# A gather-and-matmul residual kernel: the scheduler's semaphores replaced by one section with semaphores written by hand, two for each of 23 slots

## The chip, the cores and the metric

The kernel runs on one core of a Trainium2 chip. The metric is device time in microseconds, the median of several runs. The engines named below are TensorE (PE, matmuls; PEld is its weight load), VectorE (DVE), ScalarE (ACT), GpSimd (POOL) and SyncE (SP). ACT and SP do no arithmetic here: they only issue DMA transfers, each into a queue of its own, and both queues are served by the same 16 DMA engines.

## The reference

```python
def reference(x, itok_B_0_7, L0_cond_weights):
    # x: (128, 128, 1024), itok: (128,), weights: (8, 128, 128)
    w = weights[subjects]                       # (128, 128, 128), one matrix per batch entry
    out = jnp.einsum('bct,bcd->bdt', x, w)
    return x + out
```

For each of the 128 batch entries one of eight 128 x 128 matrices is chosen by an index, the entry's 128 x 1024 block is multiplied by it, and the block itself is added. x is 64 MiB, and so is the output; the weights are 512 KB. Each byte of x is read once and each byte of the output written once.

## The kernel before

The kernel takes two batch entries at a time (G = 2). A tile `xt` of 128 partitions x 2 x 1024 float32 is 1 MiB; 64 such tiles go through the kernel. The pool `xpool` has 23 buffers (BUFS, line 26), which the text calls slots: tile i lies in slot i mod 23.

At the start ACT issues two transfers: the 128 indices into `given` (line 48) and all eight weight matrices into `w_all` (line 50). DVE turns the indices into `index` (lines 54 to 59). After that the loop of line 61 does, for each tile:

- SP issues the load of the tile (line 63).
- For each of the two entries, POOL reads the index into a register and copies the chosen matrix from `w_all` to a small tile `w` (line 74; eight buffers).
- PE multiplies in two halves of 512 columns into `ps` (line 77; 4 buffers[...]).
- DVE adds the product to the tile in place (line 84).
- ACT issues the store of the tile (line 85).

The loop is a Python loop, so the program is straight code. No wait is written in the source: the framework's scheduler (Tile) orders the instructions and puts in every semaphore. For the completion of transfers issued by SP and ACT it has eight counters. It hands them out in rotation to loads and stores alike, in the order that it has planned, and a transfer is not issued until the transfer before it on the same counter has landed. In the built program loads 0 to 4 wait for nothing; load 5 waits for load 0; load 6 waits for `w_all`; load 7 for load 2; load 8 for store 0, and so on: of the 64 loads all but the first five wait for a counter that some other transfer used. From load 23 on a load also waits for the DVE's work on the tile that was in its slot. A store waits for the two additions of its tile and for its own counter. As a sequencer works in order, a waiting load holds up all later loads behind it on SP, and a waiting store all later stores on ACT. At the end SP waits for all counters, and then all engines meet in a barrier.

Of the kernel before, what the change touches and what calls it, by code (L numbers as in the profile page):

```python
# [1 line left out]

# [4 lines left out]

F32 = mybir.dt.float32
ALU = mybir.AluOpType


G = 2

N = 512

BUFS = 23


@with_exitstack
def kernel(  # L30
    ctx: ExitStack,
    tc: tile.TileContext,
    x: bass.AP,
    subjects: bass.AP,
    weights: bass.AP,
    out: bass.AP,
):
    nc = tc.nc
    B, C, T = x.shape
    S, _, D = weights.shape  # L40

    const = ctx.enter_context(tc.tile_pool(name="const", bufs=1))
    xpool = ctx.enter_context(tc.tile_pool(name="xpool", bufs=BUFS))
    wpool = ctx.enter_context(tc.tile_pool(name="wpool", bufs=8))
    psum = ctx.enter_context(tc.tile_pool(name="psum", bufs=4, space=bass.MemoryType.PSUM))

    given = const.tile([1, B], mybir.dt.int32, name="given")
    nc.scalar.dma_start(given, subjects.rearrange("(o b) -> o b", o=1))
    w_all = const.tile([C, S, D], F32, name="w_all")
    nc.scalar.dma_start(w_all, weights.rearrange("s c d -> c s d"))  # L50

    near = const.tile([1, B], mybir.dt.int32, name="near")
    nc.vector.tensor_scalar(near, given, -S, S - 1, ALU.max, ALU.min)  # L55
    wrap = const.tile([1, B], mybir.dt.int32, name="wrap")
    nc.vector.tensor_scalar(wrap, near, 0, S, ALU.is_lt, ALU.mult)  # L57
    index = const.tile([1, B], mybir.dt.int32, name="index")
    nc.vector.tensor_tensor(index, near, wrap, ALU.add)  # L59

    for b0 in range(0, B, G):
        xt = xpool.tile([C, G, T], F32, name="xt")
        nc.sync.dma_start(xt, x[b0 : b0 + G].rearrange("g c t -> c g t"))  # L63
        for g in range(G):
            b = b0 + g
            s = nc.values_load(  # L66
                index[0:1, b : b + 1],
                engines=[mybir.EngineType.Pool],
                min_val=0,
                max_val=S - 1,  # L70
                skip_runtime_bounds_check_because="the index is clamped on the chip above",
            )
            w = wpool.tile([C, 1, D], F32, name="w")
            nc.gpsimd.tensor_copy(w, w_all[:, bass.ds(s, 1), :])  # L74
            ps = psum.tile([D, T], F32, name="ps")
            for t in range(0, T, N):
                nc.tensor.matmul(  # L77
                    ps[:, t : t + N],
                    w[:, 0, :],
                    xt[:, g, t : t + N],  # L80
                    start=True,
                    stop=True,
                )
            nc.vector.tensor_tensor(xt[:, g, :], ps, xt[:, g, :], ALU.add)  # L84
        nc.scalar.dma_start(out[b0 : b0 + G].rearrange("g d t -> d g t"), xt)


# [1 line left out]
_INS = ["x", "itok_B_0_7", "L0_cond_weights"]  # L89
_OUTS = [((128, 128, 1024), "float32")]  # L90


# [20 lines left out]
```

## Time and profile before

| | |
|---|---|
| median of 3 runs | 333.06 us (332.92 to 333.22) |
| the profiled execution | 333.28 us, of which the profile's span is 331.5 us |
| bytes moved by DMA | 134.88 MB, mean 407 GB/s |
| load of one tile, SP's issue to landing (line 63) | 4.9 / 19.9 / 27.8 us (least, median, most) |
| store of one tile, ACT's issue to landing (line 85) | 4.0 / 19.8 / 27.1 us |
| weights, issue to landing (line 50) | 16.3 us |
| one addition on DVE (line 84) | 1225 ns |
| one copy of a matrix on POOL (line 74) | 294 ns |
| first load issued, first store issued, last store issued | 0.74, 25.06, 317.9 us |

The page divides the span into 40 equal slices of 8.29 us. Per slice it gives a digit of busy tenths for each engine and the rate of all DMA in GB/s. A table by stretches gives the same for any stretch of time, with the time each engine was busy in it. A table of waits says for whom an engine, or an issuing sequencer (SPq, ACTq), waited, how long in total, how many times and at most. The chain of waits follows what ended last back to what released it. A wait for several semaphores is put down to the one that came last.

### The profile page before, as it was taken

The numbers are of one execution on the slowest core, as the hardware profiler recorded it, in microseconds if no ns is written. First come the engines' busy times: TensorE is split into PE (matmuls) and PEld (weight loads), VectorE is DVE, ScalarE is ACT, GpSimd is POOL, SyncE is SP. The second block draws the span as 40 slices with busy tenths as digits, with TensorE's granted clock in tenths as the row PEclk, the third lists the DMA queues.
The fourth block names the chain that finished last, engine by engine and source line by source line (L and its number), as shares of the span: only waits on it lengthen the run. The fifth ranks groups of instructions, "written<-read, shape, count | busy, mean of one in ns | idle before, by whom it ended". The sixth has DMA issues, their size and how long they took to land.

```text
span 331.5 us, 2130 instructions
## 1 busy us (share of the span) xinstructions
PE 235.4 (71%) x512; PEld 94.5 (29%) x512; DVE 157.5 (48%) x131; POOL 37.8 (11%) x132
## 2 busy tenths in 40 slices
PE   0089999978668668668668668667877687688620
PEld 0034444423223223223223223223323233233200
DVE  0027777754454454454454454453544544545420
POOL 0031111111111111111111111110111111110000
PEclk9999999999999999999999999998899999999975
DMA  7997999999999999999999999999999999999996
GB/s 283 392 401 270 376 421 421 422 418 421 421 419 421 422 420 420 420 421 420 420 422 421 420 421 421 419 422 418 422 421 422 420 421 419 421 420 421 420 421 261
DMA packets 35870, 134.88 MB, mean 407 GB/s; under 512 B 2065, under 2 KB 3090, under 8 KB 35858
## 3 DMA queue, kind: packets, MB, share of 16 engines
q10 hardware_dynamic: 18450, 67.64, 50.2%
q1 hardware_dynamic: 17408, 67.11, 49.8%
q8 instruction: 4, 0.07, 0.1%
q14 instruction: 8, 0.07, 0.0%
HBM read 67.63 MB, written 67.11 MB: 406 GB/s over the span
## 4 chain that ended last, share of the span: by engine, by line
PE 44%; DMA 32%; DVE 14%; issue 5%; SPq 0%; POOLq 0%; POOL 0%
PE ps L77 44%; DMA xt<-in_x_dram 30%; DVE xt L84 14%; DMA out_dram<-xt 2%; DMA given<-in_itok_B_dram 0%; SPq L63 0%; POOLq L66 0%; DVE index L59 0%; DVE wrap L57 0%; DVE near L55 0%; POOLq L74 0%; POOL w L74 0%
## 5 line engine op out<-in xcount | busy, mean ns | idle before, releaser
L77 PE MATMUL ps<-xt,w 128*128 128x512 f32 x512 | 235.4, 607 | 81.2 <-DVE xt L84 55.1
L84 DVE TENSOR_TENSOR xt<-ps,xt 128x1024 f32<-128x1024 f32 x128 | 156.7, 1225 | 158.3 <-PE ps L77 158.3
L77 PEld LDWEIGHTS ps<-xt,w 128*128 128x128 f32 x512 | 94.5, 192 | 221.3 <-issue 116.2
L74 POOL COPY w<-w_all 128x128 f32 x128 | 37.6, 294 | 260.7 <-PE ps L77 242.2
L55 DVE TENSOR_SCALAR near<-given 1x128 int32<-1x128 int32 x1 | 0.2, 215 | 2.0 <-DMA given<-in_itok_B_dram 2.0
L59 DVE CUSTOM_DVE_ANT_0 index<-near,wrap 1x256 uint16<-1x256 uint16 x1 | 0.3, 280 | 0.0
L57 DVE TENSOR_SCALAR wrap<-near 1x128 int32<-1x128 int32 x1 | 0.2, 216 | 0.0
L100 POOL MEMSET const-float32-0.0<- 128x1 f32 x1 | 0.1, 98 | 0.2 <-issue 0.2
L100 POOL MEMSET const-bfloat16-1.0<- 128x1 bf16 x1 | 0.1, 101 | 0.0
L100 POOL MEMSET const-uint8-127<- 128x1 uint8 x1 | 0.1, 101 | 0.0
L100 POOL MEMSET const-float32-1.0<- 128x1 f32 x1 | 0.1, 98 | 0.0
## 6 DMA issues: line engine op xcount, KB each, us to landing
xt<-in_x_dram SPq DMA_DIRECT2D x64, 1024.0 KB, 19.9
out_dram<-xt ACTq DMA_DIRECT2D x64, 1024.0 KB, 19.8
w_all<-in_L_cond_weights_dram ACTq DMA_DIRECT2D x1, 512.0 KB, 16.3
given<-in_itok_B_dram ACTq DMA_DIRECT2D x1, 0.5 KB
```

The costliest lines, as they stand in the source:

```text
L55: nc.vector.tensor_scalar(near, given, -S, S - 1, ALU.max, ALU.min)
L57: nc.vector.tensor_scalar(wrap, near, 0, S, ALU.is_lt, ALU.mult)
L59: nc.vector.tensor_tensor(index, near, wrap, ALU.add)
L74: nc.gpsimd.tensor_copy(w, w_all[:, bass.ds(s, 1), :])
L77: nc.tensor.matmul(ps[:, t : t + N], w[:, 0, :], xt[:, g, t : t + N], start=True, stop=True,)
L84: nc.vector.tensor_tensor(xt[:, g, :], ps, xt[:, g, :], ALU.add)
L100: nc = _bacc.Bacc("TRN2", target_bir_lowering=False, num_devices=1)
```

## The change

The whole of the work goes into one critical section: a block that the scheduler leaves as it is and in which all waits are written out. All tiles are allocated once, by name: 23 x tiles, 4 tiles for the chosen matrix (there were 8 buffers), 4 in PSUM. There are 52 semaphores: for each slot one for loads and one for stores, and six for the rest of the work.

- A load of slot k waits only for the store of the tile that was in that slot before (nothing, for the first 23). All 64 loads are issued on SP, as before.
- A store waits only until the two additions of its tile are done. All stores are issued on ACT, as before.
- PE waits for the load of its slot, for the copied matrix, and for the addition four entries ago. POOL waits for the product four entries ago. DVE waits for the product.
- At the end SP waits for the last store of each slot.
- The framework adds borders to the section: at its start all engines wait for an instruction of SP, at its end for another one, before the barrier that ends the kernel.

What is computed, the order of instructions on PE, DVE, POOL, SP and ACT, and the size of every transfer stay as they were.

```diff
-BUFS = 23
+SLOTS = 23
+W_SLOTS = 4
+P_SLOTS = 4
+DMA = 16
...
-    xpool = ctx.enter_context(tc.tile_pool(name="xpool", bufs=BUFS))
-    wpool = ctx.enter_context(tc.tile_pool(name="wpool", bufs=8))
-    psum = ctx.enter_context(tc.tile_pool(name="psum", bufs=4, space=bass.MemoryType.PSUM))
+    ws = [pool.tile([C, 1, D], F32, name=f"w{i}") for i in range(W_SLOTS)]
+    xs = [pool.tile([C, G, T], F32, name=f"x{i}") for i in range(SLOTS)]
+    ps = [psum.tile([D, T], F32, name=f"ps{i}") for i in range(P_SLOTS)]
...
+    s_load = [tc.alloc_semaphore(f"s_load{i}") for i in range(SLOTS)]
+    s_store = [tc.alloc_semaphore(f"s_store{i}") for i in range(SLOTS)]
+
+    with tc.tile_critical():
...
-    for b0 in range(0, B, G):
-        xt = xpool.tile([C, G, T], F32, name="xt")
-        nc.sync.dma_start(xt, x[b0 : b0 + G].rearrange("g c t -> c g t"))
+        for i in range(NT):
+            k, turn = i % SLOTS, i // SLOTS
+            if turn:
+                nc.sync.wait_ge(s_store[k], DMA * turn)
+            nc.sync.dma_start(
+                xs[k], x[i * G : (i + 1) * G].rearrange("g c t -> c g t")
+            ).then_inc(s_load[k], DMA)
+
+        nc.gpsimd.wait_ge(s_wall, DMA)
+        for i in range(NT):
+            k, turn = i % SLOTS, i // SLOTS
+            nc.tensor.wait_ge(s_load[k], DMA * (turn + 1))
+            for g in range(G):
...
+                if b >= W_SLOTS:
+                    nc.gpsimd.wait_ge(s_product, b - W_SLOTS + 1)
+                nc.gpsimd.tensor_copy(w, w_all[:, bass.ds(s, 1), :]).then_inc(s_copied, 1)
+
+                nc.tensor.wait_ge(s_copied, b + 1)
+                if b >= P_SLOTS:
+                    nc.tensor.wait_ge(s_added, b - P_SLOTS + 1)
...
+                nc.vector.wait_ge(s_product, b + 1)
...
-        nc.scalar.dma_start(out[b0 : b0 + G].rearrange("g d t -> d g t"), xt)
+            nc.scalar.wait_ge(s_added, (i + 1) * G)
+            nc.scalar.dma_start(
+                out[i * G : (i + 1) * G].rearrange("g d t -> d g t"), xs[k]
+            ).then_inc(s_store[k], DMA)
+
+        for i in range(NT - SLOTS, NT):
+            nc.sync.wait_ge(s_store[i % SLOTS], DMA * (i // SLOTS + 1))
```

More of the change, by code (lines that the diff above doesn't have):

```diff
@@ L18 @@
 F32 = mybir.dt.float32
+I32 = mybir.dt.int32
 ALU = mybir.AluOpType
@@ L40 @@
     S, _, D = weights.shape
-    const = ctx.enter_context(tc.tile_pool(name="const", bufs=1))
-    xpool = ctx.enter_context(tc.tile_pool(name="xpool", bufs=BUFS))
-    wpool = ctx.enter_context(tc.tile_pool(name="wpool", bufs=8))
-    psum = ctx.enter_context(tc.tile_pool(name="psum", bufs=4, space=bass.MemoryType.PSUM))
-    given = const.tile([1, B], mybir.dt.int32, name="given")
-    nc.scalar.dma_start(given, subjects.rearrange("(o b) -> o b", o=1))
-    w_all = const.tile([C, S, D], F32, name="w_all")
@@ L50 @@
[L50 to L59, printed above, removed]
-    for b0 in range(0, B, G):
-        xt = xpool.tile([C, G, T], F32, name="xt")
[L63 to L82, printed above, removed]
-                )
-            nc.vector.tensor_tensor(xt[:, g, :], ps, xt[:, g, :], ALU.add)
-        nc.scalar.dma_start(out[b0 : b0 + G].rearrange("g d t -> d g t"), xt)
@@ new lines @@
+    NT = B // G
+    pool = ctx.enter_context(tc.tile_pool(name="pool", bufs=1))
+    psum = ctx.enter_context(tc.tile_pool(name="psum", bufs=1, space=bass.MemoryType.PSUM))
+    given = pool.tile([1, B], I32, name="given")
+    near = pool.tile([1, B], I32, name="near")
+    wrap = pool.tile([1, B], I32, name="wrap")
+    index = pool.tile([1, B], I32, name="index")
+    w_all = pool.tile([C, S, D], F32, name="w_all")
+    ws = [pool.tile([C, 1, D], F32, name=f"w{i}") for i in range(W_SLOTS)]
@@ new lines @@
+    xs = [pool.tile([C, G, T], F32, name=f"x{i}") for i in range(SLOTS)]
+    ps = [psum.tile([D, T], F32, name=f"ps{i}") for i in range(P_SLOTS)]
+    s_given = tc.alloc_semaphore("s_given")
+    s_wall = tc.alloc_semaphore("s_wall")
+    s_index = tc.alloc_semaphore("s_index")
+    s_copied = tc.alloc_semaphore("s_copied")
+    s_product = tc.alloc_semaphore("s_product")
+    s_added = tc.alloc_semaphore("s_added")
+    s_load = [tc.alloc_semaphore(f"s_load{i}") for i in range(SLOTS)]
+    s_store = [tc.alloc_semaphore(f"s_store{i}") for i in range(SLOTS)]
@@ new lines @@
+    with tc.tile_critical():
+        nc.scalar.dma_start(given, subjects.rearrange("(o b) -> o b", o=1)).then_inc(s_given, DMA)
+        nc.scalar.dma_start(w_all, weights.rearrange("s c d -> c s d")).then_inc(s_wall, DMA)
+        nc.vector.wait_ge(s_given, DMA)
+        nc.vector.tensor_scalar(near, given, -S, S - 1, ALU.max, ALU.min).then_inc(s_index, 1)
+        nc.vector.wait_ge(s_index, 1)
+        nc.vector.tensor_scalar(wrap, near, 0, S, ALU.is_lt, ALU.mult).then_inc(s_index, 1)
+        nc.vector.wait_ge(s_index, 2)
+        nc.vector.tensor_tensor(index, near, wrap, ALU.add).then_inc(s_index, 1)
+        nc.gpsimd.wait_ge(s_index, 3)
+        for i in range(NT):
[10 more added lines that the diff above has]
+            for g in range(G):
+                b = i * G + g
+                s = nc.values_load(
+                    index[0:1, b : b + 1],
+                    engines=[mybir.EngineType.Pool],
+                    min_val=0,
+                    max_val=S - 1,
+                    skip_runtime_bounds_check_because="the index is clamped on the chip above",
+                )
+                w, p = ws[b % W_SLOTS], ps[b % P_SLOTS]
+                if b >= W_SLOTS:
[4 more added lines that the diff above has]
+                    nc.tensor.wait_ge(s_added, b - P_SLOTS + 1)
+                for t in range(0, T, N):
+                    mm = nc.tensor.matmul(
+                        p[:, t : t + N],
+                        w[:, 0, :],
+                        xs[k][:, g, t : t + N],
+                        start=True,
+                        stop=True,
+                    )
+                mm.then_inc(s_product, 1)
+                nc.vector.wait_ge(s_product, b + 1)
+                nc.vector.tensor_tensor(xs[k][:, g, :], p, xs[k][:, g, :], ALU.add).then_inc(
+                    s_added, 1
+                )
+            nc.scalar.wait_ge(s_added, (i + 1) * G)
[4 more added lines that the diff above has]
+            nc.sync.wait_ge(s_store[i % SLOTS], DMA * (i // SLOTS + 1))
```

## The prediction

> **What bounds the kernel now.** I read the page's slices first, then a table of engines and DMA by stretch, then SP's waits, then the chain.
>
> ```profile
> PE 235.4 (71%) x512; PEld 94.5 (29%) x512; DVE 157.5 (48%) x131; POOL 37.8 (11%) x132
> ...
> DMA  7997999999999999999999999999999999999996
> GB/s 283 392 401 270 376 421 421 422 418 421 421 419 421 422 420 420 420 421 420 420 422 421 420 421 421 419 422 418 422 421 422 420 421 419 421 420 421 420 421 261
> ```
>
> No engine is full; the 16 DMA engines are, in every slice but three, and from slice 6 to slice 39 they move about 420 GB/s whatever happens. The kernel has 134.88 MB to move, and at 420 GB/s that alone is 134.88/0.420 = 321.1 us of the 331.5 us span. So the question is not who is busy but where the DMA engines were not. The slices point to the start (283), the fourth (270), the fifth (376) and the last (261). Finer stretches, columns being start:end, length, busy us and count of PE, PEld, DVE, POOL, then PE clock, DMA share, GB/s:
>
> ```profile
> 24.00:26.00 2.00, 2.00 (x6) 0.95 (x5) 1.51 (x2) 0.49 (x2) 1.00 0.38 152
> 26.00:28.00 2.00, 2.00 (x6) 0.86 (x5) 1.51 (x2) 0.29 (x1) 1.00 1.01 403
> 28.00:30.00 2.00, 2.00 (x6) 0.85 (x5) 1.51 (x2) 0.29 (x1) 1.00 0.59 236
> 30.00:32.00 2.00, 2.00 (x6) 0.95 (x5) 1.40 (x2) 0.29 (x1) 1.00 1.03 328
> 32.00:34.00 2.00, 2.00 (x6) 0.85 (x5) 1.22 (x1) 0.29 (x1) 1.00 1.02 268
> 34.00:36.00 2.00, 2.00 (x6) 0.86 (x5) 1.40 (x2) 0.37 (x2) 1.00 0.94 305
> ...
> 24.00:37.00 13.00, 13.00 (x32) 5.79 (x31) 9.55 (x8) 2.25 (x8) 1.00 0.84 290
> 37.00:326.00 289.00, 216.41 (x474) 86.13 (x472) 145.77 (x120) 32.60 (x111) 0.98 1.03 420
> ```
>
> The reader is to see one hole, 24 to 37 us, with PE busy throughout it: what is missing there is transfers, not compute. It has two halves. At 24-26 and 28-30 us the DMA engines are idle (share 0.38 and 0.59). From 30 to 36 us they count as busy but move only 268 to 328 GB/s. Why transfers are missing is in SP's own waits over the first 37 us:
>
> ```profile
> SPq L63 <- DMA out_dram<-xt: 14.6, 2, 10.5
> SPq L63 <- DMA w_all<-in_L_cond_weights_dram: 11.6, 1, 11.6
> SPq L63 <- DMA xt<-in_x_dram: 2.1, 1, 2.1
> ```
>
> SP only loads x, into 23 slots that are all still unused, and yet it waits for the weights and for stores. These are the counters: eight completion counters are shared by all transfers, and a transfer waits until the last one on its counter has landed. Load 8 shares a counter with store 0, so it isn't issued until 29.08 us (SP's timeline), though slot 8 has been empty all along. The chain of waits shows the same step for the second store:
>
> ```profile
> 27.24 1.24 DVE xt L84
> 28.47 0.02 issue
> 28.50 5.00 DMA out_dram<-xt
> 33.50 0.02 issue
> 33.51 0.37 SPq L63
> ```
>
> After 37 us SP's waits add up to far more (159.2 us for loads, 73.2 us for stores), but they cost nothing: four or so transfers lie in each queue (19.9 us from issue to landing, at one slot per 5 us), and the rate stays at 420.
>
> **What the Trainium skill says.** "DMA: Bandwidth & Descriptors", section "Anatomy of one DMA", says that the DMA engines themselves never wait on a semaphore: the issuing sequencer waits, then dispatches. That is how a wait for somebody else's store can drain the load queue here, and the trace agrees (SP waits 10.5 us, the rate falls to 152). Its section "Queues, rings and completion order" says that each DMA engine takes turns among the queues that have work, packet by packet. The trace agrees: from 40 to 318 us the load queue has 50.1% and the store queue 52.3%. So a long queue of loads should not shut out the weights or the stores. Its section "Why a DMA increments its semaphore by 16 and not by 1" recommends one semaphore for each slot in flight, for correctness; it promises no time.
>
> **The change part by part.**
> 1. *SP's waits on shared counters go.* The 23 first loads are issued back to back: SP's issue took 367 to 999 ns, so all 23 in 10 to 20 us instead of 8 by 18 us. Loads in the queue then last until 23 x 2.5 = 57 us at least (1.05 MB at 420 GB/s is 2.5 us), and the first store is issued at 25.06 us. From there a slot is loaded and stored in 2 x 2.5 = 5 us, while PE makes one in 3.43 us (1.717 us for each half between DVE's starts at 27.24, 28.96, 30.67). So stores are always at hand too. Load 23 + n waits for store n; stores land about every 5 us from 30 us on, store n at 30 + 5n, while loads, of which eight have landed by 25 us and then one every 5 us, reach load 22 + n only at 25 + 5 x (15 + n) = 100 + 5n us. SP is thus some 14 slots ahead and no wait for a slot can drain the queue. The hole of 13 us at 290 GB/s is worth 13 x (1 - 290/420) = 4.0 us. Of this, 2 x (1 - 0.38/1.03) + 2 x (1 - 0.59/1.03) = 2.1 us is idle DMA, and 2 x (92 + 152 + 115)/420 = 1.7 us is slow packets from 30 to 36 us. I take both: -4.0 us. The second is less sure: the packets slow down just when loads start again beside a store, and no row says whether a never-emptied load queue avoids that. Lower end: -2.1.
> 2. *What is late next.* After 37 us the rate is already the ceiling, so nothing there can be won. Before 24 us the DMA engines are full too (391 GB/s, where the weights' 512-byte packets are in the mix); the weights should land as before, PE starts at 18 us as before. At the end the loads finish about 8 slots ahead of the stores, as now, so the last 20 us are stores alone at 420; the last product is no limit.
> 3. *Entry into the section.* All engines now wait for one instruction of SP before they start: an instruction and a wait, at the 0.07 us that lie between the barrier's last step and the first DMA issue: +0.15.
> 4. *Exit.* Now, SP has about four steps after the last landing; changed, about eight plus one hand-over to the other engines before the final barrier. At the 0.06 to 0.08 us between the barrier's steps around 330.8 to 331.0 us: +0.35.
> 5. *Unevenness.* In the last slices the DMA engines don't end together: 383, then 104 GB/s from 326 to 330 us. That lag grew since 37 us, after the hole had let all catch up. Without the hole it grows over a tenth more: about +0.2.
> 6. *w in 4 buffers instead of 8; PSUM 4 as now.* POOL's copy takes 0.29 us, and its wait for the product of four halves ago ends 3 x 1.7 = 5 us before PE needs the copy. Nothing, hidden under PE; if it showed it would be 0.3 us per half on an engine with 1.3 us to spare per slot. Removed and moved semaphore instructions on PE, DVE and ACT (17 ns each) go with it. PE's and DVE's products run beside the DMA with 5.0 - 3.43 = 1.5 us of slack per slot.
>
> Sum: -4.0 + 0.15 + 0.35 + 0.2 = -3.3 us. On the profiled execution, 333.28 (span 331.5 and 1.8 around it), that is 330.0. The median of the runs is 0.22 lower, 333.06, which gives 329.8.
>
> **The rivals.**
> - *Half the gain.* The slow packets come back as soon as loads and stores first run side by side, whoever waited. For it: from 30 to 36 us the DMA share is 0.94 to 1.03 at only 268 to 328 GB/s, so it was not starvation. Against: store 0 ran at 403 GB/s, and mixed traffic from 37 us on at 420. Then -2.1 + 0.7 = -1.4: 331.6.
> - *The change doesn't do what it says.* The hardware itself may hold no more than five or so loads at once, so that SP stalls on issue and stores queue behind it. For it: issues made back to back took up to 999 ns, against 367 otherwise. Against: such a stall holds SP only while the DMA engines are full. If the hole stays anyway: 333.06 + 0.5 = 333.5, or unchanged if the exit is as cheap as now.
> - *Slower: the section's borders are jumps.* The skill's "Runtime: NRT & Kernel Launch", section "Instruction fetch mechanics", says that a taken branch whose target isn't in the two pages at hand stalls for a fetch. The section adds two borders, one at the entry and one at the exit, with nothing to hide behind. No row prices such a stall; the nearest is the smallest DMA at the start, 1.27 us to landing. Floor 0; three fetches in series at each border, as each engine's jump waits for SP's, would be 2 x 3 x 1.27 = 7.6, replacing the 0.5 above: 333.06 - 3.8 + 7.6 = 336.9. It decides from 3.8 us on. Against: the two borders that exist today show only the 0.07 us step. The branches go to the next block, so I take 0.
>
> **How the numbers follow.** About 0.2% (0.7 us) is what a measurement of this kernel can tell from no change. Full gain 0.70, own range 328.8 to 330.6; half the gain 0.17; no effect 0.06; slower 0.07. The low end is the full hole with free borders and an even end, 333.06 - 4.3 = 328.8; the high end takes in half the gain and a little, 331.7. The predicted time is the full gain's. Faster: 0.70 + 0.17 = 0.87; within 0.2%: 0.05 of the no-effect case; slower: 0.07 and the rest of it, 0.08.
>
> **What would show it.** Right: the fourth and fifth slices near 400 to 420 GB/s; 23 load issues within 20 us of the start; no wait of SP for the weights; weights landing near 17.6 us; first store issue near 25 us; median landing of loads far above 19.9 us, since they queue (50 us and more). The half-gain case would show slices of about 300 with a share of 1.0 right after the first store. A border's price shows as a first DMA issue after 0.74 us or as more than 1.4 us between the last landing and the end. I am wrong if the rate after 37 us is not 420 with longer queues, if the weights land much later and PE ends up last, or if the end has a gap between the last load and the stores.

## The result, and the profile after

The changed kernel takes 329.87 us (median of 4, 329.79 to 329.91) against 333.14 us for the kernel before in the same comparison (332.92 to 334.19): ratio 0.9895, 95% interval 0.9874 to 0.9916. The profiled execution took 329.91 us, with a span of 328.1.

From the page of the changed kernel: busy time by engine, then DMA share and GB/s in 40 slices of 8.2 us.

```profile
PE 233.1 (71%) x512; PEld 94.5 (29%) x512; DVE 157.5 (48%) x131; POOL 37.8 (12%) x132
...
DMA  7999999999999999999999999999999999999995
GB/s 270 391 407 413 422 420 419 423 417 420 423 419 419 422 419 419 420 422 420 420 422 420 421 420 420 420 421 422 419 421 422 417 421 422 421 419 423 421 418 239
```

The engines do what they did. The dip of the fourth and fifth slices (270 and 376 before) is gone (413 and 422). The same table by stretches as before, of the changed kernel:

```profile
24.00:26.00 2.00, 2.00 (x6) 0.95 (x5) 1.37 (x2) 0.29 (x1) 1.00 1.02 408
26.00:28.00 2.00, 2.00 (x6) 0.81 (x5) 1.23 (x1) 0.29 (x1) 1.00 1.03 412
28.00:30.00 2.00, 2.00 (x6) 0.90 (x5) 1.36 (x2) 0.30 (x2) 1.00 1.02 408
30.00:32.00 2.00, 2.00 (x6) 0.95 (x5) 1.51 (x2) 0.58 (x2) 1.00 1.03 424
...
24.00:37.00 13.00, 13.00 (x32) 5.74 (x31) 8.98 (x9) 2.20 (x8) 1.00 1.03 416
37.00:324.00 287.00, 215.19 (x476) 86.55 (x474) 146.70 (x120) 33.96 (x116) 0.97 1.03 421
```

Both halves of the hole are filled, the idle one and the slow one, and the rate afterwards is the old ceiling. SP's waits, of the changed kernel (who waited for what, us in total, times, longest):

```profile
SPq L138 <- DMA out_dram<-x: 52.6, 11, 27.6
```

Of the waits for transfers this is all that is left, and it is the wait of line 138 for the last stores. No load has to wait for a semaphore any more. What it does instead is in the row of the load's issue (times, least, median and most ns of one, first and last start):

```profile
L92 SPq DMA_DIRECT2D x<-in_x_dram x64: 422/4628/11186, 1.0 to 268.3; - x64
```

An issue took 367 to 999 ns before; now the median is 4628 ns. SP is held up by the queue itself: with about seven loads in flight the next issue ends only when one has gone through (the issues of loads 9 to 13, before the first store, end 2.4 to 2.5 us apart). The price of the change is at the end, in the rows of the closing barrier, first before and then changed (the clearing of the semaphores):

```profile
L109 POOLq EVENT_SEMAPHORE_RANGE_CLEAR  x1: 96/96/96, 331.1 to 331.1; - x1
```

```profile
L162 POOLq EVENT_SEMAPHORE_RANGE_CLEAR  x1: 352/352/352, 327.4 to 327.4; - x1
```

From the landing of the last store to the end of the span it is 1.0 us before (330.5 to 331.5) and 2.1 us after (326.0 to 328.1), and the clearing is 0.26 us of the difference. The rows of SP's last waits and of its branch out of the section, of the changed kernel:

```profile
L138 SPq EVENT_SEMAPHORE  x11: 27/28/28, 300.5 to 326.0; - x11
L72 SPq COMPARE_BRANCH  x1: 38/38/38, 326.5 to 326.5; - x1
```

### The profile page after: what moved, and what is told of

Its sections match the earlier page's. It is cut to its first block, busy times and chain, and to the rows that moved or that the text cites. A ratio compares the mean times of both kernels' runs of the same rounds, so it can differ in the third digit from the quotient of the medians.

```text
span 328.1 us, 1864 instructions
## 1 busy us (share of the span) xinstructions
PE 233.1 (71%) x512; PEld 94.5 (29%) x512; DVE 157.5 (48%) x131; POOL 37.8 (12%) x132
## 4 chain that ended last, share of the span: by engine, by line
SPq 81%; DMA 10%; PE 1%; issue 1%; DVE 0%
SPq L92 81%; DMA x<-in_x_dram 10%; PE ps L118 1%; DVE x L128 0%; SPq L162 0%; SPq L72 0%
## 5 line engine op out<-in xcount | busy, mean ns | idle before, releaser
L118 PE MATMUL ps<-x,w 128*128 128x512 f32 x512 | 233.1, 605 | 72.4 <-DMA x<-in_x_dram 53.3
L128 DVE TENSOR_TENSOR x<-ps,x 128x1024 f32<-128x1024 f32 x128 | 156.8, 1225 | 147.0 <-PE ps L118 147.0
L118 PEld LDWEIGHTS ps<-x,w 128*128 128x128 f32 x512 | 94.5, 191 | 210.2 <-issue 122.1
## 6 DMA issues: line engine op xcount, KB each, us to landing
x<-in_x_dram SPq DMA_DIRECT2D x64, 1024.0 KB, 32.9
```

Of the source, the lines that this page charges most:

```text
L118: mm = nc.tensor.matmul(p[:, t : t + N], w[:, 0, :], xs[k][:, g, t : t + N], start=True, stop=True,)
L128: nc.vector.tensor_tensor(xs[k][:, g, :], p, xs[k][:, g, :], ALU.add).then_inc(s_added, 1)
```

## The experiments

Each run's time is the median of its executions, its ratio against runs of the kernel before in the same comparison, on the same chip. The chip is not the same for all comparisons.

**The old waits put back on the first 23 loads.** What remains different from the kernel before is everything else in the rewriting.

```diff
+            gate = {5: s_load[0], 6: s_wall, 7: s_load[2], 8: s_store[0], 9: s_store[1],
+                    10: s_load[6], ..., 18: s_store[9], ..., 22: s_load[18]}.get(i)
+            if gate is not None:
+                nc.sync.wait_ge(gate, DMA)
             nc.sync.dma_start(
```

> The changed kernel, with the waits of the kernel before put back on its first 23 loads alone (loads 5 to 22 wait for the transfer that held their counter: load 5 for load 0, load 6 for the weights, load 8 for store 0, load 9 for store 1 and so on). All else as changed. Theory 1, the gain is the load queue that no longer runs dry between 24 and 37 us: the hole comes back, 13 us at about 290 GB/s, and costs the 3.9 us that it cost before: 329.9 + 3.9 = 333.8 us (333.2 to 334.2). Theory 2, the gain lies in the rest of the rewriting (stores that wait for no counter, waits by slot after load 23, deeper queues, 32.9 us to landing instead of 19.9): 329.8 to 330.4 us.

Measured: 334.92 us (16 executions, 334.06 to 335.44), ratio 1.0045 (1.0032 to 1.0057). The stretches and SP's waits of this run:

```profile
24.00:26.00 2.00, 2.00 (x5) 0.76 (x4) 0.72 (x2) 0.29 (x1) 1.00 0.47 184
26.00:28.00 2.00, 2.00 (x6) 0.94 (x5) 1.51 (x2) 0.29 (x1) 1.00 0.20 82
28.00:30.00 2.00, 2.00 (x6) 0.80 (x6) 1.51 (x2) 0.29 (x1) 1.00 1.02 406
30.00:32.00 2.00, 2.00 (x6) 0.92 (x5) 1.33 (x2) 0.29 (x1) 1.00 0.58 234
32.00:34.00 2.00, 2.00 (x6) 0.93 (x5) 1.23 (x1) 0.29 (x1) 1.00 1.03 291
...
24.00:37.00 13.00, 13.00 (x31) 5.68 (x30) 8.73 (x8) 2.06 (x7) 1.00 0.75 254
```

```profile
SPq L95 <- DMA out_dram<-x: 41.8, 6, 12.1
SPq L95 <- DMA x<-in_x_dram: 28.2, 7, 5.9
SPq L95 <- DMA w_all<-in_L_cond_weights_dram: 11.7, 1, 11.7
```

The hole is back, with the waits for the weights and the stores, and all of the gain is gone: Theory 1 holds, Theory 2 falls. But it is 1.1 us more than I had said. The hole is larger than before, 13 x (1 - 254/420) = 5.1 us against 4.0, and the first store is issued at 26.7 us, not at 25.1. Whether the one explains the other is what the next run asks.

**The same, with POOL's first read of the index ahead of its wait for the weights.** In the changed kernel POOL waits for the weights before it reads the first index; before, it read the index at 2.85 us and only its copy waited.

```diff
-        nc.gpsimd.wait_ge(s_wall, DMA)
...
+                if b == 0:
+                    nc.gpsimd.wait_ge(s_wall, DMA)
                 nc.gpsimd.tensor_copy(w, w_all[:, bass.ds(s, 1), :]).then_inc(s_copied, 1)
```

> As the run with all 18 old waits put back, but POOL waits for the weights only after it has read the first index, as in the kernel before. In that run the first store began 1.7 us later than before, since POOL's read of the index now stood behind the weights. Theory: that delay, and nothing else, made the hole of that run 5.1 us instead of 4.0, so the hole shrinks by about 1 us: 333.7 to 334.1 us against 334.92. Rival, the section itself makes the hole worse: 334.7 to 335.1.

Measured: 334.41 us (333.27 to 334.72), ratio 1.0026 (1.0011 to 1.0042). The first store is issued at 25.8 us, the hole is 13 x (1 - 271/420) = 4.6 us. So the order of index and weights goes with about half of the extra microsecond; some 0.5 us stays unexplained, in a run whose executions spread over 1.4 us.

**One of the old waits alone.**

```diff
+            gate = {8: s_store[0]}.get(i)
+            if gate is not None:
+                nc.sync.wait_ge(gate, DMA)
```

> The changed kernel with one wait put back: load 8 waits until store 0 has landed. Theory 1a, the hole is idle DMA and the restart of the loads costs nothing more: the queue is dry from about 25.4 us to the first packets of store 0 at 26.8 and from their end at 29.4 to the restart at 30.2, about 2.1 us: 332.0 us, with packets at full rate (over 390 GB/s) from 30.5 us on. Theory 1b, restarting loads beside a store slows the packets: 30 to 36 us again at 260 to 330 GB/s, 1.7 us more: 333.7 us. Theory 2, one wait early on doesn't matter: 329.9 us.

Measured: 335.05 us (334.14 to 335.65), ratio 1.0046 (1.0031 to 1.0061). One wait, on one transfer out of 128, costs 5 us against the changed kernel. That is 1.3 us more than the dearest of the theories had said. The profiled execution was the fastest of the ten (334.14 us), so about 0.9 us of the median's loss is in no trace. The stretches of this run:

```profile
24.00:26.00 2.00, 2.00 (x6) 0.80 (x6) 1.23 (x1) 0.29 (x1) 1.00 0.49 193
26.00:28.00 2.00, 2.00 (x6) 0.92 (x5) 1.34 (x2) 0.30 (x1) 1.00 0.71 287
28.00:30.00 2.00, 2.00 (x6) 0.93 (x5) 1.51 (x2) 0.57 (x2) 1.00 0.61 238
30.00:32.00 2.00, 2.00 (x6) 0.80 (x6) 1.51 (x2) 0.32 (x2) 1.00 1.03 375
32.00:34.00 2.00, 2.00 (x6) 0.93 (x5) 1.51 (x2) 0.29 (x1) 1.00 0.93 199
34.00:36.00 2.00, 2.00 (x6) 0.92 (x5) 1.48 (x2) 0.29 (x1) 1.00 1.04 371
36.00:38.00 2.00, 2.00 (x6) 0.80 (x6) 1.23 (x1) 0.29 (x1) 1.00 0.98 336
```

Idle until 30 us, and then, with the loads issued again from 29.8 us on, the DMA engines are busy and slow once more: Theory 1b. The trace's packets show whose they are: at first no load moves (the first packet of load 8 comes at 33.5 us), and it is the packets of the store under way, of 4096 bytes, that take a median of 329 to 395 ns from 32 to 34 us, for 160 otherwise. From 34 us on the loads' packets are back at a median of 160 ns, but single ones still take up to 784 ns. So the slow packets belong to the hole; they are not something that happens at 30 us in any case. That they vanish with it in the changed kernel is what the prediction had counted on.

**A dry load queue in the middle.** Is it the restart of the loads that is slow?

```diff
+            if i == 40:
+                nc.sync.wait_ge(s_load[39 % SLOTS], DMA * (39 // SLOTS + 1))
```

> The changed kernel with one wait in the middle: load 40 waits until load 39 has landed, so that the load queue runs dry once, around 180 us, while several stores are queued. Theory 1b, a restart of loads beside a running store slows the packets by itself, as it did at 30 to 36 us: a stretch of 4 us or so at 200 to 350 GB/s, 1.7 us more: 331.6 us. Theory 1c, the packets slow down only where both queues are nearly empty: the stores fill the gap, nothing is lost: 329.9 us (329.7 to 330.2).

Measured: 329.56 us (329.42 to 329.95), ratio 0.989 (0.9873 to 0.9906): nothing lost. The stretches of this run:

```profile
180.00:182.00 2.00, 0.93 (x3) 0.10 (x1) 1.51 (x2) 0.29 (x1) 1.00 1.03 424
182.00:184.00 2.00, 1.79 (x4) 0.87 (x5) 0.20 (x1) 0.00 (x0) 1.00 1.02 420
184.00:186.00 2.00, 1.91 (x5) 0.57 (x3) 1.27 (x2) 0.30 (x1) 1.00 1.01 416
186.00:188.00 2.00, 0.00 (x0) 0.00 (x0) 1.18 (x1) 0.29 (x1) 1.00 1.03 424
```

From 182 to 184 us no load moves at all (load 40 is issued at 182.26 us, and its first packet comes at 185.8); PE stops soon after for want of tiles; and the DMA engines do not notice, since the stores queued on ACT take the whole rate. Theory 1b in its general form falls: a restart of loads is not slow by itself. Here a dry load queue cost nothing, since the other queue filled in.

**Stores held until four are ready, beside the one old wait.**

```diff
-            nc.scalar.wait_ge(s_added, (i + 1) * G)
+            nc.scalar.wait_ge(s_added, max(i + 1, 4) * G)
```

> The changed kernel with load 8 waiting for store 0, as in the run with one wait put back, and the first four stores held until all four tiles are done, so that stores 1 to 3 are queued when the loads restart. The hole is longer by design (about 25.4 to 37 us without transfers, some 9 us of it new), so the total says nothing; what is asked is the rate in the 6 us after the restart of the loads, some 0.5 us after store 0 has landed. Theory 1c, packets slow down only where a load restarts beside a single store with nothing queued behind it: 390 GB/s and more. Theory 1d, the first restart of loads beside stores is slow whatever is queued: 200 to 350 GB/s for about 4 us.

Measured: a single execution, 343.32 us. Load 8 is issued at 40.3 us. The stretches of this run:

```profile
40.00:42.00 2.00, 2.00 (x6) 0.84 (x5) 1.42 (x2) 0.36 (x2) 1.00 1.03 397
42.00:44.00 2.00, 2.00 (x6) 0.95 (x5) 1.51 (x2) 0.53 (x2) 1.00 1.05 377
44.00:46.00 2.00, 2.00 (x6) 0.86 (x5) 1.51 (x2) 0.19 (x1) 1.00 0.94 219
46.00:48.00 2.00, 2.00 (x6) 0.85 (x5) 1.51 (x2) 0.40 (x2) 1.00 1.04 420
```

Neither theory has it. The slow stretch is there, but later and half as long. Again it is the stores' packets that slow down (a median of 318 ns from 44 to 45 us), though three more stores lay queued behind the one under way. So queued stores alone do not prevent it, and what makes these packets slow stays open.

**Four loads in flight, and two.** These ask whether depth matters, or only that the queue is not empty.

```diff
+            if i >= 4:        # 2 in the second run
+                nc.sync.wait_ge(s_load[(i - 4) % SLOTS], DMA * ((i - 4) // SLOTS + 1))
```

> The changed kernel with at most four loads in flight all along: load i also waits until load i - 4 has landed. Theory 1, it is enough that the load queue is never empty: four loads of 2.5 to 5 us each last 10 to 20 us, so nothing is lost, 329.9 us (329.6 to 330.3), with loads at 10 to 20 us from issue to landing. Theory 2, the deep queue (6 or 7 loads in flight after the change, about 4 before) gives the gain: above 331 us.

> The changed kernel with at most two loads in flight: load i also waits until load i - 2 has landed. If a load that is still moving (2.5 us) covers the landing and the next issue (about 1 to 1.4 us together), nothing is lost: 329.9 to 330.5 us. If the queue runs dry between loads, the first 25 us (8 loads alone) lose up to 1 us each and restarts beside stores slow the packets: 335 us or more.

Measured: four, 329.74 us (329.67 to 329.99), ratio 0.9888 (0.986 to 0.9916), loads 19.9 us from issue to landing as before the change; two, 330.48 us (329.70 to 330.50), ratio 0.9916 (0.99 to 0.9933), 9.9 us. Four in flight lose nothing, so the deeper queue (32.9 us) is not the gain. Two lose some 0.6 us in three of four executions; the profiled one is the fourth, so no trace shows where.

**12 slots instead of 23.**

```diff
-SLOTS = 23
+SLOTS = 12
```

> The changed kernel with 12 slots instead of 23, so 24 slot semaphores instead of 46. Theory 1, the slots are not what was short: queues stay non-empty, the DMA rate stays at 420 GB/s, and the exit with its clearing of semaphores (0.35 us for the clear alone after, 0.10 before) gets some 0.2 to 0.5 us shorter: 329.4 to 329.8 us. Rival, 23 slots are needed since a slot lives 33 us in the load queue, 5 us in compute and 32 us in the store queue, 70 us or 14 slots: SP waits for stores often and the DMA runs dry: above 331 us.

Measured: 329.72 us (329.62 to 329.91), ratio 0.9887 (0.9859 to 0.9915). Slots were not short: loads now did wait for slots (load 12 was issued at 35.3 us, not at 19.9), and the rate stayed at 421 GB/s. The clearing at the end took 226 ns in place of 352. The time is 0.15 us lower, which is no more than the spread of the executions.

**The kernel before with larger transfers.** If bytes in flight at the start are all that matters, eight shared counters are enough once each covers 2 MiB.

```diff
-G = 2
+G = 4
-BUFS = 23
+BUFS = 11
```

> The kernel before, waits by the scheduler and its eight shared counters, but four batch entries per tile (2 MiB transfers, 11 slots, the same memory). In its program the first load that waits for a store is load 7, when 14 MiB have been asked for instead of 8. Theory 1, the hole comes from the bytes that eight counters allow in flight: 14 MiB last to about 45 us, longer than store 0 takes to land, so the hole goes without any section, and its 1.3 us of borders with it: 328.6 to 329.4 us. Rival, shared counters cost by themselves whatever the size, or the last 2 MiB tile is exposed at the end: 331 us or more.

Measured: 329.06 us (329.02 to 329.48), ratio 0.9878 (0.9861 to 0.9894). From its page:

```profile
GB/s 272 391 409 409 420 420 421 419 420 423 422 419 421 420 422 420 420 422 420 422 420 421 420 421 421 421 421 423 420 422 420 421 418 422 423 420 421 421 422 280
```

No hole, with the scheduler's own waits. Load 7 still waits for store 0, until 44.26 us, but load 6 lands only at 48.5, so the load queue doesn't run dry meanwhile. The same size of tile in the hand-written section:

```diff
-G = 2
+G = 4
-SLOTS = 23
+SLOTS = 11
```

> The changed kernel with four batch entries per tile (2 MiB transfers), 11 slots and so 22 slot semaphores. The same size of transfer under the scheduler's counters took 329.06 us. Theory, what is left between the two ways of waiting is the section's borders, 1.3 us in the profile, less what fewer semaphores to clear give back (0.1 to 0.2 us): 329.9 to 330.3 us if larger transfers cost and gain nothing, 329.4 us at the least. Rival, the gain of the larger transfers is their own: 328.5 us or less.

Measured: 329.34 us (329.28 to 329.93), ratio 0.9879 (0.9863 to 0.9896). So the larger tile seems to help the section too, by about 0.5 us, which I had not expected; and what the section then costs against the scheduler is 0.3 us by the medians, less than the 0.7 us that entry (0.2) and exit (0.5) differ by in the profiles of the two. These runs were made on different chips, and the profiled execution of this one was the slowest of its four, so this isn't settled.

Last, the changed kernel and the kernel before with 2 MiB tiles, on one chip:

> The changed kernel again, on the same chip as the run below. 329.7 to 330.0 us, as in its first measurement.

> The kernel before with 2 MiB tiles and 11 slots again, beside the changed kernel on one chip. If it is really the faster of the two (329.06 against 329.87 us, measured on different chips), it is 0.5 to 1.0 us below the changed kernel here too; if the difference was one between chips, the two are within 0.2 us.

Measured: the changed kernel 329.90 us (329.82 to 330.03), ratio 0.9903 (0.9882 to 0.9924); the kernel before with 2 MiB tiles 329.01 us (328.96 to 329.29), ratio 0.9877 (0.9856 to 0.9898). The executions of the two do not overlap: two changed numbers in the old kernel beat the rewriting by 0.9 us. By the run before this one, some 0.5 us of that may be the larger transfers' own gain.

## Why the prediction was right

The time came out at 329.87 us where 329.8 was said, and by the mechanism that was said. Two terms of the sum were off, the exit by 0.75 us and the unevenness by 0.8 us, in opposite directions. That they cancel is luck; without it the total would have been off by some 0.8 us, a quarter of the gain.

- *SP's waits on shared counters* (-4.0): 13 x (416 - 290)/420 = 3.9 us. The runs with the old waits put back carry it: one wait on load 8 alone takes the whole gain back. Both halves came, the idle one (2.1) and the slow packets (1.7), so the rival "half the gain" is out.
- *How* it goes was partly wrong. I had 23 loads issued within 20 us and then queueing 50 us and more. In fact SP's issues block at about 7 MiB in flight: the 23rd load was issued at 63 us, and the median load took 32.9 us. The rival that the hardware holds only a few loads was right about the limit and wrong about its effect. The run with four in flight shows why it doesn't matter. Nor did the long load queue leave the first store alone, as I had concluded from the queues' taking turns: store 0, issued at 25.97 us, got its first packet at 29.6. Only from then on did the two queues share evenly.
- *What is late next* (nothing): right for the rate after 37 us and for the end. But "PE starts at 18 us as before" was not so: PE starts at 19.1. The weights land 0.3 us later, and POOL's read of the first index was moved behind the wait for them, a step that I had missed (with the read moved back, in the second run, PE starts at 18.6). It costs nothing here, since the loads fill the DMA engines meanwhile; in the runs with a hole it did show, by about half a micro-second.
- *Entry* (+0.15): 0.2, the first load is issued at 0.96 us instead of 0.74.
- *Exit* (+0.35): 1.1. I counted steps at the pace of the barrier and left out the clearing of 52 semaphores instead of a few (+0.26 us) and a pause of 0.43 us between SP's last wait (326.02) and its branch out of the section (326.46). The rest, some 0.4 us, is the steps that I did count. The pause lies where the branch rival expected a stall, but it is not the price of the border as such: with four and with two loads in flight, at the same border, 0.06 us lie there. What it is stays open.
- *Unevenness* (+0.2): -0.6. Before, 0.97 MB were left at 326 us, which is 2.3 us at 420, and the last packet ended at 330.1, so 1.8 us were lost to engines that finished early. After, 0.21 MB were left at 324, 0.5 us, and the last ended at 325.7: 1.2 us. I had taken the lag to grow with the length of undisturbed running. These two profiles don't bear that out.
- *w in 4 buffers* (nothing): not tried by itself; PE's and DVE's rows hardly differ in the page (605 and 1225 ns of one against 607 and 1225).

With 0.2 us less lost between 37 and 310 us, -3.9 + 0.2 + 1.1 - 0.6 - 0.2 = -3.4, the difference of the spans (331.5 and 328.1).

## What to carry to other kernels

When a kernel is bound by DMA, look for the stretch in which the DMA engines are not full, and ask of each load at that point what it is really waiting for: with completion counters shared by loads and stores, a load can wait for a store that has nothing to do with it, and a single such wait at the start, while the store queue is still empty, costs what nothing later gives back. A wait that emptied the load queue in the middle of this kernel cost nothing, because queued stores took the whole rate. Before writing semaphores by hand, try larger transfers: bytes in flight were what the counters limited, and doubling the tile filled the hole too and left the kernel 0.9 us faster than the section did.

## What the runs showed of the hardware

- SP's queue took about seven loads of 1 MiB; then each issue lasted until one had gone through, 4.63 us at half the DMA rate against 0.37 us for an issue into a queue with room.
- A transfer that is issued while the other queue is full doesn't start at once, though the queues share evenly later (51.2% of the 16 engines' time each from 40 to 300 us). The changed kernel's store 0 is issued at 25.97 us; the DMA queues from 26 to 29.4 us show packets of the load queue (q1) and none of the store queue:

```profile
q1 hardware_dynamic: 355, 1.39, 102.4%
...
out_dram<-x ACTq DMA_DIRECT2D x1, 1024.0 KB, 9.2
```

  Its first packet came at 29.6 us and it took 9.2 us to land; before, with the load queue dry, it took 4.0. In the other direction it is the same: load 40 of the run with a dry load queue in the middle got its first packet 3.5 us after its issue.
- Kernels with the hole vary more from execution to execution (332.18 to 334.35 us for the kernel before in its longest series, of 25) than those without (329.82 to 330.03 us for the changed kernel in its longest, of six). That points to the hole as the source of the variation; no trace shows it.
- The packets of a store, of 4096 bytes, took about twice their 160 ns for some 2 us when loads were issued again beside the first stores (a median of 329 to 395 ns from 32 to 34 us in the run with one wait). Three more stores queued behind did not prevent it (219 GB/s from 44 to 46 us); in the middle of the kernel, beside about six queued stores, it did not happen (416 GB/s and more from 180 to 188 us). The cause is open.
